# Gate and up products turned to features by tokens, in a Flamingo block on one Trainium2 core

## Chip, cores and metric

The kernel runs on one core of one Trainium2 chip. The metric is device time in microseconds (us) per execution. The kernel before has a median of 458.49 us over 3 runs (458.45, 458.49 and 459.89).

The five engines are named as in the profile: PE is TensorE's matmul stream and PEld its weight loads, DVE is VectorE, ACT is ScalarE, POOL is GpSimd, SP is SyncE, which here only issues DMAs.

## What is computed

The input x has 16 batches of 128 tokens with 512 features. For every batch the kernel computes a gated cross-attention and a gated feed-forward network with Hadamard-rotated, quantized products:

```
x = x + tanh(g_xattn) * attention(layernorm(x), ctx, ctx)      # 32 query heads, 8 key heads, D = 16
x = x + tanh(g_ffn)   * ffn(layernorm(x))

def h_bitlinear(v, w):        # w becomes -1, 0 or 1 times its mean magnitude
    r = hadamard(v)           # along the features, 512 or 2048 of them
    s = 127 / max(max(abs(r)), 1e-5)          # one scale per token
    return (clip(round(r * s), -128, 127) / s) @ ternary(w).T

def ffn(v):                   # w_gate, w_up: 2048 x 512; w_down: 512 x 2048
    return h_bitlinear(silu(h_bitlinear(v, w_gate)) * h_bitlinear(v, w_up), w_down)
```

## The kernel before

One batch of 128 tokens fills the 128 partitions, so there are 16 batches b = 0 to 15, and every batch goes through the same steps. The steps are Python generators: each call runs one up to its next `yield`. A text, `ORDER`, lists 1,489 such calls, and a wrapper (`InOrder`) keeps the instructions of PE, DVE, ACT, POOL and SP in the order in which the list issues them. So each engine works through a fixed queue, and an instruction that waits holds up all that stand behind it on its engine. Steps of several batches are interleaved in the list.

The attention steps of one batch are `moments_q`, `normed`, `q_transposed`, `scores` (PE writes scores `sc`, DVE reduces them to maxima `mx`), `split_max`, `max_turned`, `weights` (PE writes `sT`, ACT takes the exponential `ex`), `summed` (`av`) and `residual` (PE transposes `tpo`, DVE divides, POOL adds into x).

The feed-forward steps of one batch are:

- `moments_h`: mean and variance of x (DVE `stf`, `mvf`), then the inverse root on POOL (`vef`, `rstdf`, `nmf`).
- `in_norm`: ACT writes the normalized row `hn`, POOL does two butterfly levels (`hb`, `hn`).
- `in_turned`, `in_hadamard`: PE transposes 4 blocks (`tph`), a copy to SBUF, PE multiplies by the 128 x 128 Hadamard matrix into `z`.
- `in_scale`, `in_quant`: the maximum per token and its reciprocal (`ae`, `re`), POOL's `dq`, the rounded row `qe` by ACT, a DMA that transposes it (`qTe`).
- `gate.b.m`, `up.b.m` for m = 0, 1: `product` writes a tile of 128 tokens by 1024 features: 8 matmuls with 512 columns each, the activations `qTe` as weights of the array and the ternary weights streaming. ACT takes silu of the gate tile with the token's scale `dq`, giving `sg`; DVE multiplies the up tile, `dq` and `sg` to `h`.
- `hidden_transposed.b.n` for n = 0 to 3: PE turns 4 blocks of `h` (`tpf`), ACT or DVE copies them to SBUF (`hT`).
- `hadamard.b.n`: PE multiplies by the Hadamard matrix into `y`, ACT or DVE copies to `za`.
- `butterfly.b.1/2/4` on DVE (`zb`, `za`), `magnitudes` on ACT, `out_scale` and `out_quant` on DVE (`qf`), a transposing DMA (`qTf`), a cast, and `out_down` (16 matmuls into `yo`, then `res` on DVE and a store).

The last digit of a step such as `hadamard.3.2.1` chooses the engine of its copy: 0 or none is ACT, 1 is DVE.

Other steps are `load_*`, `mag_*`, `mean_*`, `whole_*` and `clipped_*`, which load and ternarize the weights early in the list; `table.i.k`, an activation table load ahead of exponentials (k = 0) or silu (k = 1); and `warm.i.n`, n matmuls whose result nobody reads.

Two PSUM pools matter. `ps_s` has 2 buffers of 1024 values per partition and serves `sc`, `sT`, `gate` and `up`; `ps_x` has 4 buffers of 512 values and serves the rest.

Of the kernel before, what the change touches and what calls it, by code (L numbers as in the profile page):

```python
# [8 lines left out]
F32 = mybir.dt.float32  # L9
BF16 = mybir.dt.bfloat16  # L10
# [13 lines left out]
load_kv0 load_aux warm.0.12 load_x1 load_g.1 fetch.2 moments_q.0 load_g.0 load_g.3 table.0.0  # L24
gates_in load_sel moments_q.0 normed.0 q_transposed.0 load_g.2 q_transposed.0 mag_g.1 scores.0.1
fetch.4 load_u.2 moments_q.1 moments_q.1 warm.1.6 scores.0.1 scores.0.1 normed.1 moments_q.2
scores.0.0 moments_q.2 load_u.3 q_transposed.1 scores.0.0 warm.2.8 q_transposed.1 values_in.1
mag_g.0 scores.0.0 values_in.0 moments_q.3 load_u.1 scores.1.1 mag_g.3 moments_q.3 warm.3.4
scores.1.1 load_u.0 warm.4.2 scores.1.1 split_max.0 max_transposed.0.1 normed.2 max_transposed.0.1
scores.1.0 sel_in mag_g.2 q_transposed.2 scores.1.0 scores.1.0 warm.5.6 mean_g q_transposed.2  # L30
normed.3 weights.0.1 mean_g whole_g.3 whole_g.1 warm.6.8 weights.0.1 weights.0.1 whole_g.0 load_d.0
load_d.3 weights.0.0 moments_q.5 moments_q.5 summed.0.1 mag_u.3.1 weights.0.0 load_d.2 weights.0.0
split_max.1 mag_u.2 scores.2.1 clipped_g.0 max_transposed.1 scores.2.1 summed.0.0.1 max_transposed.1
summed.0.1 residual.0.1 scores.2.1 whole_g.2.1 summed.0.0.1 weights.1.0 residual.0.1 moments_q.4
q_transposed.3.1 weights.1.0 residual.0.0 q_transposed.3.1 weights.1.0 residual.0.0 residual.0.0
mag_u.0 scores.2.0 moments_q.4 summed.1.0 residual.0.1 summed.1.0 scores.2.0 scores.2.0 mag_u.1
residual.1.0 split_max.2 weights.1.1 moments_h.0 clipped_g.3 residual.1.0 moments_h.0
max_transposed.2.1 weights.1.1 fetch.6 mean_u warm.7.8 max_transposed.2.1 mean_u weights.1.1
load_d.1 whole_u.1 in_norm.0 scores.3.1 normed.4 in_norm.0 scores.3.1 whole_u.0.1 q_transposed.4
summed.1.1 in_norm.0 scores.3.1 q_transposed.4 whole_u.3 residual.1.0 normed.5 scores.3.0  # L40
in_turned.0 scores.3.0 in_turned.0 values_in.3 whole_u.2.1 scores.3.0 in_hadamard.0 in_scale.0
split_max.3 weights.2.1 summed.1.1 clipped_u.3 residual.1.1 moments_q.6 moments_q.6 weights.2.1
weights.2.1 max_transposed.3.1 q_transposed.5.1 clipped_g.2 residual.1.1 in_quant.0 weights.2.0
in_quant.0 max_transposed.3.1 moments_q.7 residual.1.1 mag_d.0.1 weights.2.0 values_in.2 summed.2.1
weights.2.0 moments_h.1 moments_h.1 normed.6 weights.3.1 summed.2.1 q_transposed.5.1 clipped_u.1
residual.2.1 weights.3.1 clipped_u.2 q_transposed.6.1 summed.2.0 weights.3.1 residual.2.1 in_quant.0
clipped_g.1 weights.3.0 in_norm.1 mag_d.2.1 summed.2.0 in_norm.1 summed.3.1 fetch.8 weights.3.0
residual.2.0 weights.3.0 in_scale.0 gate.0.0 residual.2.0 residual.2.0 clipped_u.0 mag_d.1.1 up.0.0
table.1.1 gate.0.0 in_norm.1 summed.3.1 mag_d.3 gate.0.1 residual.2.1 q_transposed.6.1 moments_q.7
up.0.0 in_turned.1.1 hidden_transposed.0.1 in_turned.1.1 mean_d up.0.1 moments_h.2  # L50
hidden_transposed.0.1 mean_d moments_h.2 in_hadamard.1 gate.0.1 up.0.1 values_in.4 summed.3.0
values_in.5 summed.3.0 in_scale.1 scores.4.0 moments_q.8 in_scale.1 in_norm.2 hidden_transposed.0.3
scores.4.0 in_quant.1 in_norm.2 hadamard.0.1 residual.3.0 hidden_transposed.0.3 in_quant.1
scores.4.0 hadamard.0.1 hadamard.0.3 moments_q.8 whole_d.0.1 residual.3.0 scores.5.1 residual.3.1
in_norm.2 hadamard.0.3 hidden_transposed.0.2.1 scores.5.1 in_quant.1 in_turned.2 whole_d.3.1
hidden_transposed.0.0 residual.3.1 gate.1.1 scores.5.1 residual.3.0 residual.3.1
hidden_transposed.0.0 moments_q.9 in_turned.2 up.1.1 gate.1.1 moments_h.3 hidden_transposed.0.2.1
normed.7 moments_h.3 in_hadamard.2 up.1.1 hadamard.0.2.1 in_scale.2 scores.4.1 in_quant.2.1
in_scale.2 moments_q.9 hidden_transposed.1.3 in_quant.2.1 hadamard.0.0 in_norm.3 in_norm.3
scores.4.1 scores.4.1 gate.1.0 hadamard.0.0 whole_d.1.1 hadamard.0.2.1 split_max.4 butterfly.0.1  # L60
up.1.0 gate.1.0 in_quant.2.1 in_norm.3 max_turned.4 hidden_transposed.1.2 whole_d.2.1 up.1.0
gate.2.0 clipped_d.1 hidden_transposed.1.2 up.2.0 hidden_transposed.1.3 gate.2.0 butterfly.0.1
butterfly.0.2 hidden_transposed.1.0 hadamard.1.2 up.2.0 hadamard.1.3.1 hidden_transposed.1.0
butterfly.0.2 butterfly.0.4 hadamard.1.2 weights.4.0 in_turned.3 table.2.0 weights.4.0
hidden_transposed.2.0.1 hadamard.1.3.1 hadamard.1.0.1 butterfly.0.4 weights.4.0
hidden_transposed.1.1 in_turned.3 hidden_transposed.2.0.1 weights.4.1 magnitudes.0 clipped_d.3
hadamard.1.0.1 summed.4.0 clipped_d.0 weights.4.1 weights.4.1 in_hadamard.3 out_scale.0
hidden_transposed.1.1 gate.2.1 out_quant.0.1 out_scale.0 hadamard.2.0.1 in_scale.3 out_quant.0.1
table.3.1 gate.2.1 summed.4.1 hadamard.2.0.1 in_scale.3 summed.4.0 scores.5.0 out_quant.0.0.1
values_in.6 in_quant.3 summed.4.1 in_quant.3 residual.4.0 scores.5.0 hadamard.1.1 out_quant.0.0.1  # L70
residual.4.1 residual.4.0 up.2.1 scores.5.0 residual.4.0 in_quant.3 residual.4.1 split_max.5
gate.3.0 up.2.1 hadamard.1.1 out_quant.0.1 butterfly.1.1 butterfly.1.1 residual.4.1 max_turned.5
hidden_transposed.2.1 up.3.0 hidden_transposed.2.1 gate.3.0 out_quant.0.0.1 hadamard.2.1 up.3.0
hidden_transposed.2.3 hadamard.2.1 butterfly.1.2 hidden_transposed.3.0 hidden_transposed.2.3
weights.5.1 butterfly.1.2 hadamard.2.3 table.4.0 weights.5.1 butterfly.1.4 hidden_transposed.3.1
weights.5.1 q_transposed.7 hadamard.2.3 scores.6.0 hidden_transposed.3.0 moments_h.4
hidden_transposed.3.1 summed.5.1 butterfly.1.4 magnitudes.1 scores.6.0 hidden_transposed.2.2
scores.6.0 hadamard.3.0.1 moments_h.4 in_norm.4 out_scale.1 scores.6.1 q_transposed.7 summed.5.1
hadamard.3.1 out_scale.1 in_norm.4 residual.5.1 hadamard.3.1 scores.6.1 scores.6.1 gate.3.1
hidden_transposed.2.2 in_norm.4 hadamard.3.0.1 residual.5.1 hadamard.2.2.1 table.5.1 gate.3.1  # L80
out_quant.1.0 split_max.6 max_turned.6 in_turned.4 weights.5.0 hadamard.2.2.1 butterfly.2.1
out_down.0.0 table.6.0 weights.5.0 in_turned.4 butterfly.2.1 out_quant.1.0 weights.5.0 up.3.1
clipped_d.2 butterfly.2.2 out_down.0.1 up.3.1 out_quant.1.0 out_quant.1.1.1 hidden_transposed.3.3
summed.5.0 weights.6.1 hidden_transposed.3.3 butterfly.2.2 out_quant.1.1.1 summed.5.0 out_down.0.1
butterfly.2.4 hidden_transposed.3.2 weights.6.1 residual.5.0 in_hadamard.4 hidden_transposed.3.2
butterfly.2.4 weights.6.1 hadamard.3.2 residual.5.0 magnitudes.2 weights.6.0 in_scale.4 residual.5.0
residual.5.1 hadamard.3.3 weights.6.0 out_scale.2 out_down.1.0 weights.6.0 out_quant.1.1.1
hadamard.3.3 moments_h.5 in_quant.4 scores.7.1 out_quant.2.1.1 normed.8 moments_h.5 in_quant.4
hadamard.3.2 summed.6.0 scores.7.1 summed.6.1 scores.7.1 out_down.1.1 in_scale.4 values_in.7
summed.6.1 butterfly.3.1 in_norm.5 in_quant.4 in_norm.5 summed.6.0 scores.7.0 out_down.1.1  # L90
residual.6.0 scores.7.0 q_transposed.8 q_transposed.8 in_norm.5 residual.6.1 scores.7.0 gate.4.0
values_in.8 residual.6.1 split_max.7 residual.6.0 out_down.0.1 up.4.0 table.7.1 gate.4.0
out_quant.2.0.1 residual.6.0 gate.4.1 out_quant.2.0.1 up.4.0 residual.6.1 butterfly.3.1 max_turned.7
hidden_transposed.4.1 up.4.1 hidden_transposed.4.1 butterfly.3.2 gate.4.1 in_turned.5 up.4.1
fetch.10 out_quant.2.1.1 hidden_transposed.4.0 hadamard.4.1 hidden_transposed.4.0 butterfly.3.2
butterfly.3.4 in_turned.5 weights.7.0 table.8.0 weights.7.0 weights.7.0 butterfly.3.4
# [164 lines left out]
def flamingo_kernel(  # L261
# [355 lines left out]

    def absmax_scale(b: int, name: str, amax, norm: float):  # L620

# [372 lines left out]
```

## Time and profile before

| | |
|---|---|
| median of the runs | 458.49 us (458.45 to 459.89) |
| span of the profiled execution | 456.3 us, first to last instruction |
| between the span and the median | 2.2 us |
| PE busy | 441.8 us, 97% of the span |
| DVE busy | 416.8 us, 91% |
| ACT busy | 324.2 us, 71% |
| POOL busy | 174.8 us, 38% |
| TensorE clock granted | full (1.000) |

The profile comes from one execution with a span of 456.3 us; no separate device time is listed for that execution, so the 2.2 us that lie around the span are taken from the median. Busy time is the time in which at least one instruction of the engine is under way. Matmuls overlap in the array: the duration of one is longer than the step from it to the next, so costs on PE are taken from steps, not from durations. All lines of the kernel appear as L249, the line of the `InOrder` wrapper, so groups are told apart by the names of their tiles.

### The profile page before, as it was taken

What the parts mean: (1) busy time and instruction counts of PE and PEld (TensorE: products, weight loads), DVE (VectorE), ACT (ScalarE), POOL (GpSimd) and SP (SyncE); (2) the same over time, 40 slices, a digit from 0 to 9 for tenths busy, and PEclk for the clock granted to TensorE, in tenths of its full rate; (3) what the DMA queues carried; (4) which work ended last, traced back from release to release, by engine and by line L of the source; (5) the groups of instructions that cost most, each with busy time, mean ns of one, the idle gap of its engine ahead of it and who ended that gap; (6) DMA issues with size and microseconds to landing.
All of it is one profiled execution on the core that took longest, in us unless ns stands there. A gap on an engine that the chain in (4) does not pass through costs nothing.

```text
span 456.3 us, 8222 instructions
## 1 busy us (share of the span) xinstructions
PE 441.8 (97%) x3191; PEld 266.2 (58%) x3228; DVE 416.8 (91%) x624; ACT 324.2 (71%) x391; POOL 174.8 (38%) x316
## 2 busy tenths in 40 slices
PE   7999899999999999999999999999999999999996
PEld 3534447665665465666555665565556656576862
DVE  4898998999999999999999899989789999989995
ACT  4779897788787677596977878575776748645641
POOL 3315656512241713237274632358152542251000
PEclk9999999999999999999999999999999999999999
DMA  8998220003011153051131513030023503111331
GB/s 283 404 410 272 90 82 13 13 12 59 13 31 29 36 139 83 13 153 33 36 57 36 139 23 70 2 88 18 1 57 47 71 0 62 45 23 37 69 70 69
DMA packets 59350, 36.38 MB, mean 80 GB/s; under 512 B 47792, under 2 KB 52144, under 8 KB 58288
## 3 DMA queue, kind: packets, MB, share of 16 engines
q1 hardware_dynamic: 59312, 35.86, 29.2%
q8 instruction: 25, 0.41, 0.4%
q14 instruction: 13, 0.11, 0.1%
HBM read 20.12 MB, written 4.19 MB: 53 GB/s over the span
## 4 chain that ended last, share of the span: by engine, by line
PE 74%; DVE 10%; DMA 6%; POOL 3%; ACT 3%; issue 2%; SPq 1%; DVEq 0%; POOLq 0%; ACTq 0%
PE y L249 13%; PE yo L249 11%; PE up L249 10%; PE gate L249 10%; PE sT L249 7%; PE tpf L249 6%; PE sc L249 6%; PE av L249 6%; DMA wq_down<-in_w_up 3%; DVE mx L249 3%; PE z L249 3%; PE tpo L249 2%; DVE zb L249 2%; DMA wst_gate<-in_w_gate 2%; DVE h L249 1%
## 5 line engine op out<-in xcount | busy, mean ns | idle before, releaser
L249 DVE TENSOR_REDUCE mx<-sc 128x8 f32<-128x1024 f32 x64 | 75.5, 1217 | 8.6 <-PE sc L249 8.3
L249 PEld LDWEIGHTS <-qTe 128*128 128x128 bf16 x512 | 50.0, 98 | 52.9 <-DVE mx L249 0.8
L249 DVE TENSOR_TENSOR zb<-za 128x1024 f32<-128x1024 f32 (+1 forms) x62 | 72.7, 1198 | 1.4 <-ACT za L249 0.7
L249 PE MATMUL y<-aux,hT 128*128 128x128 f32 x544 | 72.5, 278 | 0.3 <-ACT za L249 0.2
L249 PEld LDWEIGHTS y<-aux,hT 128*128 128x128 f32 x544 | 66.7, 192 | 9.8 <-issue 3.5
L249 ACT ACTIVATE ex<-sT 128x1024 f32<-128x1024 f32 x64 | 62.7, 1026 | 12.1 <-PE sT L249 11.7
L249 PE MATMUL up<-wq_up,qTe 128*128 128x512 bf16 x247 | 60.0, 379 | 0.5
L249 PE MATMUL gate<-wq_gate,qTe 128*128 128x512 bf16 x239 | 59.6, 379 | 0.9
L249 PE MATMUL yo<-wq_down,qTf 128*128 128x512 bf16 x245 | 58.7, 379 | 0.6
L249 POOL TENSOR_TENSOR x<-x,ga 128x256 f32<-128x256 f32 x32 | 30.1, 946 | 47.7 <-DVE ga L249 47.5
L249 DVE SCALAR_TENSOR_TENSOR h<-up,dq,sg 128x1024 f32<-128x1024 f32 x32 | 41.0, 1281 | 7.7 <-ACT sg L249 4.7
L249 ACT ACTIVATE sg<-gate,dq 128x1024 f32<-128x1024 f32 x32 | 35.7, 1116 | 15.5 <-PE gate L249 12.4
L249 PE MATMUL sc<-kb,qT 32*128 32x256 f32 x512 | 40.5, 402 | 1.6 <-ACT qT L249 0.7
L249 PEld LDWEIGHTS <-qTf 128*128 128x128 bf16 x256 | 24.4, 98 | 29.1 <-issue 1.3
L249 PE MATMUL sT<-qT,kb 32*128 32x512 f32 x256 | 40.8, 640 | 0.5 <-DVE h L249 0.2
L249 DVE TENSOR_TENSOR za<-zb 128x1024 f32<-128x1024 f32 (+1 forms) x38 | 39.3, 1059 | 0.2
L249 DVE CUSTOM_DVE_ANT_0 qf<-zb,rf 128x1024 int16<-128x1024 f32 (+1 forms) x32 | 38.9, 1224 | 0.2
L249 ACT COPY hT<-tpf 128x512 f32<-128x512 f32 x45 | 26.1, 591 | 18.2 <-PE tpf L249 16.5
L249 PE MATMUL tpf<-ident,h 128*128 128x128 f32 x256 | 38.0, 277 | 0.4 <-DVE h L249 0.2
L249 PEld LDWEIGHTS tpf<-ident,h 128*128 128x128 f32 x256 | 29.0, 141 | 14.2 <-issue 6.9
L249 POOL TENSOR_TENSOR hb<-hn 128x256 f32<-128x256 f32 x32 | 25.8, 828 | 28.4 <-ACT hn L249 18.1
L249 PEld LDWEIGHTS sc<-kb,qT 32*128 32x128 f32 x512 | 25.1, 184 | 17.8 <-issue 6.5
(128 smaller groups left out, 728.1 us busy)
## 6 DMA issues: line engine op xcount, KB each, us to landing
wst_gate<-in_w_gate SPq DMA_DIRECT2D x4, 1024.0 KB, 9.6
wst_down<-in_w_down SPq DMA_DIRECT2D x4, 1024.0 KB, 12.7
out<-res SPq DMA_DIRECT2D x16, 256.0 KB, 2.2
x<-in_x SPq DMA_DIRECT2D x7, 512.0 KB, 4.1
kb<-in_kb SPq DMA_DIRECT2D x8, 256.0 KB, 4.1
wq_down<-in_w_up SPq DMA_DIRECT2D x2, 1024.0 KB, 14.1
wst_up<-in_w_up SPq DMA_DIRECT2D x2, 1024.0 KB, 15.2
kv<-in_kv SPq DMA_DIRECT2D x8, 128.0 KB, 3.9
```

The source lines that it names most:

```text
L249: ins = f(*args, **kwargs)
```

## The change

Five things are changed together.

1. `product` swaps its operands: the ternary weights are loaded into the array in blocks of 128 x 128, the activations stream with 128 columns. The tile comes out as features by tokens, 32 matmuls with 128 columns in place of 8 with 512. `hidden_transposed` and its copy are gone. The scale of a token now lies along the free axis, so a new step `spread` puts it on all partitions (one matmul with the identity, one copy), and `gate` multiplies by it on DVE, with silu on ACT afterwards, from SBUF to SBUF. `up` multiplies two tensors.
2. `moments_h` and ACT's `hn` are gone. `in_norm` works on x itself; the mean falls out with one zeroed column of the Hadamard matrix (`had_mid`), and the new step `in_power` takes the squares of `z` on ACT with a running sum, then five small instructions on POOL.
3. POOL takes some of the weights' rounding: 4 of the 12 `whole_*` (ACT had 7 of them and has 3 now, DVE keeps 5) and 6 of the 12 `clipped_*` (all were DVE's).
4. For the batches 0 to 13 the end of `out_down` is an ACT copy with the scale and a POOL addition in place of one DVE instruction.
5. Many steps have more `yield`s, and `ORDER` is a new list of 1,696 calls. In it, the choice of engine for `hadamard`'s 64 copies is 57 on ACT and 7 on DVE (before: 42 and 22). The `table` and `warm` steps are the same 26 and 8, in other places; three `warm` steps, with 16 matmuls, stand at the end of the list.

```diff
...
+    had_mid = const.tile([P, P], F32, name="had_mid")
...
         def whole(c: int, k: int = 0):
             w = part[c].bitcast(I16)
-            if k == 0:
-                nc.vector.tensor_scalar(w, st[c], inv, None, ALU.mult)
+            if k == 1:
+                nc.scalar.activation(w, st[c], AF.Copy, scale=inv)
             else:
-                nc.scalar.activation(w, st[c], AF.Copy, scale=inv)
+                (nc.vector, nc.gpsimd)[k // 2].tensor_scalar(w, st[c], inv, None, ALU.mult)
-        def clipped(c: int):
-            nc.vector.tensor_scalar(part[c], part[c].bitcast(I16), -1.0, 1.0, ALU.max, ALU.min)
+        def clipped(c: int, k: int = 0):
+            (nc.vector, nc.gpsimd)[k].tensor_scalar(part[c], part[c].bitcast(I16), -1.0, 1.0, ALU.max, ALU.min)
...
-    def moments_h(b: int):
-        return moments(b, "f")
     def in_norm(b: int):
-        hn = w1.tile([P, KC, P], F32, tag="hn", name=f"hn_{b}")
-        layer_norm(b, "f", hn.rearrange("p c f -> p (c f)"), xs[b])
-        src = hn
+        src = xs[b].rearrange("p (c f) -> p c f", c=KC)
...
+    def in_power(b: int):
+        z = zes[b].rearrange("p c f -> p (c f)")
+        ins[b] = w1.tile([P, E], I16, tag="qe", name=f"qe_{b}")
+        power = tiny.tile([P, 1], F32, tag="power", name=f"power_{b}")
+        nc.scalar.activation(ins[b].bitcast(BF16), z, AF.Square, accum_out=power)
+        yield
+        nc.gpsimd.tensor_scalar(ve, power, 1.0 / E**2, EPS, ALU.mult, ALU.add)
+        yield
+        nc.gpsimd.tensor_tensor(rstd, ve, mhalf, ALU.pow)
+        yield
+        nc.gpsimd.tensor_scalar(dq, wsc[:, 0:2], a, rstd, ALU.mult, ALU.mult)
+        yield
+        nc.gpsimd.tensor_tensor(root, ve, half, ALU.pow)
+        yield
+        nc.gpsimd.tensor_scalar(floor, root, rs["e", b], wsc[:, 3:4], ALU.mult, ALU.mult)
+    def spread(b: int, k: int = 0):
+        row = ps_x.tile([P, P], F32, tag="x", name=f"row_{b}")
+        nc.tensor.matmul(
+            row, lhsT=dqs[b][:, 0:1].to_broadcast([P, P]), rhs=ident, start=True, stop=True
+        )
+        yield
+        rows[b] = w2.tile([P, P], F32, tag="row", name=f"rowb_{b}")
+        copies[k](rows[b], row)
...
     def product(b: int, m: int, w: str):
-        gu = ps_s.tile([P, 2, 512], F32, tag="s", name=f"{w}_{b}_{m}")
-        for j in range(2):
+        gu = ps_s.tile([P, 8, P], F32, tag="s", name=f"{w}_{b}_{m}")
+        for j in range(8):
             for c in range(KC):
                 nc.tensor.matmul(
-                    gu[:, j, :], lhsT=ins[b][:, c, :],
-                    rhs=wq[w][c][:, (2 * m + j) * 512 : (2 * m + j + 1) * 512],
+                    gu[:, j, :],
+                    lhsT=wq[w][c][:, (8 * m + j) * P : (8 * m + j + 1) * P],
+                    rhs=ins[b][:, c, :],
                     start=(c == 0), stop=(c == KC - 1),
                 )
     def gate(b: int, m: int):
         gu = product(b, m, "gate")
         yield
-        sgs[b, m] = w1.tile([P, 2, 512], F32, tag="sg", name=f"sg_{b}_{m}")
-        nc.scalar.activation(sgs[b, m], gu, AF.Silu, scale=dqs[b][:, 0:1])
+        sg = w3.tile([P, 8, P], F32, tag="sg", name=f"sg_{b}_{m}")
+        nc.vector.tensor_tensor(sg, gu, rows[b].unsqueeze(1).to_broadcast([P, 8, P]), ALU.mult)
+        yield
+        nc.scalar.activation(sg, sg, AF.Silu)
     def up(b: int, m: int):
         gu = product(b, m, "up")
         yield
-        h = w2.tile([P, 2, 512], F32, tag="h", name=f"h_{b}_{m}")
-        nc.vector.scalar_tensor_tensor(
-            h, gu, dqs[b][:, 1:2], sgs.pop((b, m)), ALU.mult, ALU.mult
-        )
+        h = sgs.pop((b, m))
+        nc.vector.tensor_tensor(h, gu, h, ALU.mult)
...
-    def hidden_transposed(b: int, n: int, k: int = 0):
-        h = hs[b, n // 2][:, n % 2, :]
-        tp = ps_x.tile([P, 4, P], F32, tag="x", name=f"tpf_{b}_{n}")
-        for c in range(4):
-            nc.tensor.transpose(tp[:, c, :], h[:, c * P : (c + 1) * P], ident)
-        yield
-        hT = w2.tile([P, 4, P], F32, tag="hT", name=f"hT_{b}_{n}")
-        copies[k](hT, tp)
...
     def out_down(b: int, k: int, parts: int = 2):
...
-            nc.vector.scalar_tensor_tensor(res, y, scs[b], xs[b], ALU.mult, ALU.add)
+            if b < 14:
+                nc.scalar.activation(res, y, AF.Copy, scale=scs[b])
+                yield
+                nc.gpsimd.tensor_tensor(res, res, xs[b], ALU.add)
+            else:
+                nc.vector.scalar_tensor_tensor(res, y, scs[b], xs[b], ALU.mult, ALU.add)
             yield
             nc.sync.dma_start(out[b], res)
```

## Prediction

> **What bounds it now.** I read the page first, then the busy time by stretch, the chain of waits, the groups by form, and last single tiles.
>
> ```profile
> PE 441.8 (97%) x3191; PEld 266.2 (58%) x3228; DVE 416.8 (91%) x624; ACT 324.2 (71%) x391; POOL 174.8 (38%) x316
> 100.00:200.00 100.00, 99.40 (x741) 60.19 (x748) 96.52 (x144) 75.34 (x93) 31.34 (x56) 1.00 0.24 56
> 200.00:300.00 100.00, 99.32 (x730) 59.30 (x738) 94.41 (x134) 75.57 (x93) 47.23 (x76) 1.00 0.24 57
> 300.00:400.00 100.00, 98.82 (x716) 60.47 (x724) 92.97 (x139) 70.64 (x84) 41.73 (x65) 1.00 0.24 40
> ```
>
> The columns of the last three lines are the stretch, its length, and the busy time of PE, PEld, DVE, ACT and POOL. PE hardly stops from 100 to 400 us, but DVE is only 3 to 7 us per 100 behind. Work taken from PE alone buys little: DVE is next. The chain agrees: 74% of it is PE, and the transposes that the change removes have their share.
>
> ```profile
> 425.00 1.51 PE gate L249 x7
> 426.51 0.44 PE tpf L249 x4
> 429.11 3.57 PE y L249 x32
> 447.33 0.39 PE L249 MATMUL tpf_q<-ident,qf 128*128 128x128 bf16 x4
> L249 PE MATMUL tpf_q<-ident,qf x16: 219/219/230, 447.3 to 450.6; 128*128 128x128 bf16 x16
> ```
>
> These give steps on PE (start, length, what, count; then a tile's durations, lowest, median, highest). A bf16 matmul with 512 columns takes 1.51/7 = 0.216 us, an f32 transpose 0.44/4 = 0.110, an f32 pass with 128 columns 3.57/32 = 0.112. Four bf16 matmuls with 128 columns, each behind its own weight load, last 0.39 with one lasting 0.219, so their step is (0.39 - 0.219)/3 = 0.057.
>
> ```profile
> L249 DVE SCALAR_TENSOR_TENSOR h<-up,dq,sg 128x1024 f32<-128x1024 f32 x32 | 41.0, 1281 | 7.7 <-ACT sg L249 4.7 <-PE up L249 2.6
> L249 ACT ACT_TABLE_LOAD x26 | 33.4, 1283 | 1.2 <-PEq L984 0.7
> L249 ACT COPY hT<-tpf 128x512 f32<-128x512 f32 x45 | 26.1, 591 | 18.2 <-PE tpf L249 16.5 <-PE y L249 1.4 <-ACT ex L249 0.3
> L249 DVE TENSOR_TENSOR zb<-za x62: 684/1218/1750, 90.4 to 442.6; 128x1024 f32<-128x1024 f32 x58, 128x512 f32<-128x512 f32 x4
> L249 POOL TENSOR_TENSOR x<-x,ga x32: 720/730/1697, 36.9 to 396.3; 128x256 f32<-128x256 f32 x32
> ```
>
> The first three are groups (busy us and mean ns, then idle time before); the last two are tiles. DVE's butterfly goes from its median of 1.218 to 1.750 and POOL's addition from 0.730 to 1.697, so the two do get in each other's way, POOL mostly being the one delayed.
>
> **The change, part by part.** All sums are against the span of 456.3 us; 2.2 us lie around it.
>
> PE. Gone: 256 transposes, 256 x 0.110 = 28.2. The 64 gate and up tiles cost 8 x 0.216 = 1.73 each; they become 32 x 0.057 = 1.82, together +6.1. No run of more than four such matmuls in a row is in the trace. The nearest row on the other side is the f32 pass at 0.112, which has the same 128 columns but the slower weight load (192 ns against 98); the floor is 1.73/32 = 0.054, the streaming of the same columns. I take 0.057, because type and load are the same. `spread`: 16 matmuls of two f32 passes, 3.6. Sum: 441.8 - 28.2 + 6.1 + 3.6 = 423.3.
>
> The Trainium skill speaks against this step: its page "TensorE: Matmul & The Clock Gate", section "Back-to-back issue gap", gives about 81 ns per matmul in a sustained stream of weight loads and matmuls with 128 columns. With it the 64 tiles would cost +55.3 and PE would come to 472.5. The same sentence gives 131 ns for 512 columns, where this trace has 216, so I let the trace decide.
>
> DVE. Gone: 19 copies `hT` 12.7, `stf` and `mvf` 13.8, 14 of the 16 `res` 14 x 0.740 = 10.4, 15 copies of `y` now on ACT 15 x 0.681 = 10.2, 6 clips 6 x 0.682 = 4.1, other copies on balance 2.6: together 53.8. New: the gate tile's multiplication, 32 times, between 1.218 (butterfly, SBUF) and 1.281 (`h`, same PSUM tile); I take 1.25, 40.0. `h` itself drops to that too, -1.0. Nine copies of the token row, 0.28 each from the cast of 256 values (0.283): 2.5. Sum: 416.8 - 53.8 + 41.5 = 404.5.
>
> ACT. Gone: `hT` 26.1, `hn` 13.1, four `whole` 8.0, silu from SBUF some 1.9. New: 15 copies of `y` 8.9, 16 squares 14.1 (0.693 as `qe` on the same tile, and 0.19 for the accumulator's read), 14 scaled `res` 9.7, seven token rows 2.2, other copies 3.9. Sum: 313.9. Then the table loads. Before, all 26 loads are the 26 `table` steps, and every one stands where the function changes. Following ACT's queue in the new list, the function still changes 26 times, but 25 of the uses find the wrong table behind the last `table` step. So there are between 26 loads (misplaced ones dropped) and 51, and ACT has between 313.9 and 313.9 + 25 x 1.283 = 346.0. I take 51, since each of the 26 steps did become a load before. ACT then is at 79% of 440 us: mostly hidden, not everywhere.
>
> POOL. Gone: `vef`, `rstdf`, `nmf`, `dq`, 30.6. New: five small instructions per batch, 0.47 + 0.58 + 0.46 + 0.58 + 0.46, 40.8 in all; 14 additions of 512 values, twice 0.730, 21 (to 27 by the mean of 0.946); ten roundings of 2048 values, each between 2.1 (four of `m_pad`'s memset of 512 at 0.524) and 9.8 (sixteen of `v_pad`'s 128 at 0.610). I take 4, below the addition's rate (eight times 0.730 = 5.8) as there is one input less: 40. Sum 246, from 227 to 310, under POOL's span either way. The cover is the long wait that POOL has now. Without it: five of the ten stand ahead of the first gate product, where the list has 32 us of other POOL work in 64 us; at 9.8 they would add 32 + 49 - 64 = 17 us. DVE's butterflies may be held by the long additions; the whole excess of the 58 butterflies over their median is 0.8 us now, so I price this at 0 to 4 and take 1, within the rounding of the sum.
>
> Waits. `gate` on DVE waits for PE and the token row; silu waits for it; `h` waits for silu. Behind the waiting `h` stand maxima, butterflies and rounding, on which PE's `ps_s` buffers and the stores depend. In the new list DVE has 0.7 to 11.2 us of other work between a tile's scale and its `h`, and only in 2 of 32 cases less than silu's 1.1; a table load of 1.28 ahead of silu is covered in most. The chain of `in_power` (a square, three POOL steps, one matmul, one copy, some 3 us) stands ahead of the gate tile's multiplication in the list, for several batches by one step only, so part of the 19 below is its wait. On SP, stores are moved behind later loads and transposes; their issue takes about 0.5 each, and SP is nowhere near full. The three `warm` steps at the end take 16 x 0.216 = 3.5 beside the last `res` and store (3.7 from the last `yo` to the end now): 0 to +1, I take 0.
>
> Sum of the parts. DVE becomes the fuller engine relative to what stops it. Its idle time now is 39.5: 10.9 up to 60 us (loads), 5.6 from 440 us on, 23.0 between. Head and tail stay. Of the 23.0, waits for PE are the largest part (`mx` for `sc` 8.3 over the run), and PE gets slack; against that stands the new silu in the middle of DVE's work. I keep four fifths, 19. 404.5 + 10.9 + 5.6 + 19 = 440, with 2.2 around it 442. From PE's side: 423.3 with its present idle of 14.5 gives 437.8, 440 with the 2.2. Both ends meet, so I predict 442, with 434 to 452 as this case's own range.
>
> **Rivals.**
>
> 1. *Slower: the short matmuls don't keep their step.* 2048 matmuls pay every ns. PE reaches its present 441.8 when the step is (1.73 x 64 + 24.6)/2048 = 0.066 us; from there the transposes are paid back. Halfway to the f32 row, 0.084, PE has 441.8 - 28.2 + 61.4 + 3.6 = 478.6, and with 14.5 and 2.2 the time is 495. For it: no long run in the trace, and twice 32 instructions per tile where 16 were. Against it: the measured 0.057, and weight loads of 98 ns that lie beside matmuls. Chance 0.10.
> 2. *ACT gives it back.* Between the first products of batches 3 and 4 the list holds 44 us of ACT work with all loads, against 37 on PE and 39 on DVE; ahead of the first product ACT has 58 (54 before). With two fifths of 25 x 1.283 = 32.1 us on the path, 13, the time is 455; it is level with now when half of it, 16, is. For it: exponentials empty the two `ps_s` buffers, so a load ahead of them stops PE. Against it: ACT idles 29% now, and a load can run while ACT waits. Chance 0.22, of it 0.10 faster, 0.05 same, 0.07 slower.
> 3. *Better packing.* With DVE's middle idle at 10 the time is 433. For it: PE's slack of some 18 us. Against it: three engines above 79%, in fixed queues. Chance 0.10.
>
> The forecast itself has 0.58. A measurement tells some 0.3% (1.4 us) from no change. Faster: 0.58 + 0.10 + 0.10 = 0.78; same 0.05; slower 0.10 + 0.07 = 0.17. The range 430 to 463 leaves out rival 1 and the edges of the others.
>
> **What would show it.** Steps of the gate and up matmuls at 0.057, 32 per tile; `tpf`, `hT`, `hn`, `stf` gone; DVE busy near 404 and above 91% of the span, PE near 423; some 50 table loads; POOL's roundings near 4 us each. The prediction is wrong if DVE's idle time rises well above 36 us, with `h` waiting for silu or `ex` behind table loads, or if the matmul step exceeds 0.066.

## The result: 508.7 us, a tenth slower

The changed kernel has a median of 508.66 us over 4 runs (507.2 to 511.5), against 459.18 us for the kernel before in the same comparison (4 runs). The ratio is 1.1085, with a 95% interval of 1.1048 to 1.1123. The prediction, 442 us, was wrong by sign and lies 67 us off, outside its range.

The profiled execution has a span of 505.4 us. These lines answer to those shown of before. First the page's busy times, then the busy time by stretch (stretch, its length, busy PE, PEld, DVE, ACT, POOL with counts, granted clock, DMA share, GB/s):

```profile
PE 450.8 (89%) x4520; PEld 318.1 (63%) x4540; DVE 425.8 (84%) x576; ACT 342.0 (68%) x421; POOL 311.0 (62%) x359
```

```profile
0.00:100.00 100.00, 77.01 (x625) 44.14 (x626) 72.80 (x105) 60.29 (x75) 74.95 (x93) 0.86 0.49 177
100.00:200.00 100.00, 88.80 (x962) 66.42 (x962) 84.12 (x104) 73.96 (x89) 73.00 (x69) 0.97 0.11 25
200.00:300.00 100.00, 93.83 (x995) 66.62 (x998) 88.68 (x119) 74.31 (x92) 59.15 (x74) 0.98 0.22 57
300.00:400.00 100.00, 93.43 (x951) 65.13 (x960) 87.42 (x117) 68.79 (x89) 54.03 (x74) 0.97 0.23 50
```

No engine is full any more. From 100 to 400 us PE has 89 to 94 us per 100 where it had 99, DVE 84 to 89 where it had 93 to 97. DVE's idle time is 505.4 - 425.8 = 79.6 us, against 39.5 before. PE's busy time is 450.8 us, above the 441.8 of before, though the change takes work off it. Part of that is the clock, which was full before. Now its mean is 0.956, so some 22 us' worth of full clock are lost, in six stretches, the longest in this one (the third column from the end is the granted clock):

```profile
20.00:40.00 20.00, 18.30 (x106) 8.23 (x107) 14.05 (x24) 13.56 (x18) 13.48 (x6) 0.66 0.96 371
```

Added up over the trace, 44.4 us of the span run at half clock, and PE is busy for 36.0 of them.

The steps of the new products, from the chain of waits (start, length, what, count):

```profile
272.68 3.57 PE gate L256 x64
```

3.57/64 = 0.056 us, as predicted. The Trainium skill's 81 ns per matmul of this kind ("TensorE: Matmul & The Clock Gate", "Back-to-back issue gap"), which the prediction had weighed, isn't seen here, in runs of 32 or 64.

Groups by form (busy us, mean ns, idle time before them and what ended it):

```profile
L256 DVE TENSOR_TENSOR sg<-gate,rowb 128x1024 f32<-128x1024 f32 x32 | 38.9, 1218 | 4.2 <-PE gate L256 3.9
L256 DVE TENSOR_TENSOR sg<-up,sg 128x1024 f32<-128x1024 f32 x32 | 38.6, 1216 | 13.8 <-ACT sg L256 12.2 <-PE up L256 1.4
L256 ACT ACT_TABLE_LOAD x48 | 61.6, 1283 | 2.2 <-PEq L1040 0.7 <-PE sT L256 0.7
L256 DVE TENSOR_TENSOR zb<-za 128x1024 f32<-128x1024 f32 x58 | 78.4, 1384 | 7.1 <-ACT za L256 6.6
L256 POOL TENSOR_SCALAR wq_down<-wq_down 128x2048 bf16<-128x2048 int16 x3 | 21.2, 7079 | 0.1
L256 POOL TENSOR_SCALAR wq_down<-wst_down,inv_down 128x2048 int16<-128x2048 f32 x2 | 10.9, 5444 | 0.0
```

The second line is `h`: it waits 12.2 us for silu, before 4.7. DVE's butterfly takes 1384 ns on average, its median being still 1.22 us. A clip on POOL takes 7.08 us, a rounding 5.44. The waits that have grown (who waits for whom: us in total, times, longest); the first line is of before, the others of the changed kernel:

```profile
DVE mx L249 <- PE sc L249: 8.3, 12, 2.2
DVE mx L256 <- PE sc L256: 24.5, 18, 6.0
ACT ex L256 <- PE sT L256: 20.5, 21, 3.3
PEld tph L256 <- POOL hn L256: 12.8, 6, 7.8
DVE sg L256 <- ACT sg L256: 12.2, 8, 2.9
```

DVE waits for PE's scores 24.5 us, before 8.3, and PE waits for POOL's `hn`. PE in turn waits for all three: its idle time that ended with another engine's work is 17.7 us for ACT, 15.2 for POOL and 14.4 for DVE, where before it was 3.1, 1.3 and 3.6 (added up over the two traces).

And how POOL and DVE meet, from the timeline (start, length, engine, instruction):

```profile
73.09 7.57 POOL L256 TENSOR_SCALAR wq_up<-wq_up 128x2048 bf16<-128x2048 int16 x1
75.51 5.70 DVE L256 TENSOR_SCALAR wq_up<-wq_up 128x2048 bf16<-128x2048 int16 x1
...
423.97 2.11 POOL L256 TENSOR_SCALAR dq<-wsc,ae,rstdf 128x2 f32<-128x2 f32 x1
```

DVE's clip, whose least duration is 0.69 us, starts inside POOL's and ends at 81.21, 0.55 us after POOL's end at 80.66. In the third line an instruction on two values per partition takes POOL 2.11 us. The Trainium skill ("SBUF — State Buffer", "SBUF: two separate sides") says that certain DVE instructions and POOL's take a common pair of ports as an exclusive lock for a whole instruction; the first two lines agree with it.

### The profile page after: what moved, and what is told of

Its sections match the earlier page's. It is cut to its first block, busy times and chain, and to the rows that moved or that the text cites. A ratio compares the mean times of both kernels' runs of the same rounds, so it can differ in the third digit from the quotient of the medians.

```text
span 505.4 us, 10935 instructions
## 1 busy us (share of the span) xinstructions
PE 450.8 (89%) x4520; PEld 318.1 (63%) x4540; DVE 425.8 (84%) x576; ACT 342.0 (68%) x421; POOL 311.0 (62%) x359
## 4 chain that ended last, share of the span: by engine, by line
PE 28%; DVE 21%; ACT 11%; POOL 5%; issue 4%; DMA 3%; ACTq 0%; DVEq 0%; POOLq 0%
PE y L256 6%; DVE zb L256 5%; PE yo L256 5%; DVE qf L256 4%; PE sT L256 4%; PE gate L256 4%; DVE za L256 4%; DVE mx L256 3%; DVE sg L256 3%; ACT L256 3%; PE sc L256 3%; PE up L256 2%; ACT ex L256 2%; DMA qTf<-qf 2%; PE av L256 2%
## 5 line engine op out<-in xcount | busy, mean ns | idle before, releaser
L256 DVE TENSOR_REDUCE mx<-sc 128x8 f32<-128x1024 f32 x64 | 75.4, 1216 | 24.6 <-PE sc L256 24.5
L256 PE MATMUL y<-aux,sg 128*128 128x128 f32 x544 | 75.2, 285 | 1.7 <-DVE sg L256 1.7
L256 PEld LDWEIGHTS y<-aux,sg 128*128 128x128 f32 x544 | 67.4, 196 | 13.5 <-issue 9.4
L256 PE MATMUL gate<-qTe,wq_gate 128*128 128x128 bf16 x1024 | 63.0, 222 | 2.0 <-DVE mx L256 1.2
L256 PEld LDWEIGHTS <-wq_gate 128*128 128x128 bf16 x1024 | 60.6, 99 | 6.0 <-issue 4.7
L256 PE MATMUL up<-qTe,wq_up 128*128 128x128 bf16 x1024 | 61.6, 219 | 2.2 <-ACT ex L256 1.2
L256 PEld LDWEIGHTS <-wq_up 128*128 128x128 bf16 x1024 | 59.0, 98 | 3.3 <-issue 2.5
L256 DVE TENSOR_TENSOR sg<-up,sg 128x1024 f32<-128x1024 f32 x32 | 38.6, 1216 | 13.8 <-ACT sg L256 12.2
L256 ACT COPY za<-y 128x512 f32<-128x512 f32 x53 | 30.2, 590 | 26.1 <-PE y L256 24.1
L256 DVE TENSOR_TENSOR sg<-gate,rowb 128x1024 f32<-128x1024 f32 x32 | 38.9, 1218 | 4.2 <-PE gate L256 3.9
L256 ACT ACTIVATE sg<-sg 128x1024 f32<-128x1024 f32 x32 | 33.6, 1057 | 11.7 <-DVE sg L256 11.4
```

The costliest lines, as they stand in the source:

```text
L256: ins = f(*args, **kwargs)
```

## The experiments

Theories, by the letters used in the expectations: A, POOL's roundings hold the head, and DVE by the ports; B, table loads hold ACT; C, the new order and its longer chains; D, half clock in the head; E, POOL's other long instructions hold DVE; F, DVE is simply full; G, the layout frees PE; H, the chain gate, DVE scale, silu, `h` stops the fixed queues; R, the token row does. Every time is the median of its runs; "list" is the text `ORDER`. e9, e10, e11 and e14 to e17 leave out the token's scale, wholly or in part, so they don't compute the block; they show only what a piece costs.

**The roundings, the tables, the clock (e1 to e5).** The ten steps on POOL go back to DVE (`clipped`) and ACT (`whole`):

```diff
-clipped_g.0.1 ... whole_g.2.2
+clipped_g.0 ... whole_g.2.1
```

> The changed kernel with its ten POOL roundings back on the engines of before (6 clips on DVE, 4 whole on ACT), the list of steps otherwise as changed. Theory A (POOL's roundings of 5.4 to 7.6 us each hold up the head, and DVE by the shared port): the first gate product comes some 20 us earlier, DVE's butterflies fall from 1.38 to near 1.24 us mean, time 478 to 487 us. Theory B (table loads hold up ACT): at least 500 us. Theory C (the new order and the longer chain gate, scale, silu, up are what costs): 495 to 505 us.

The 26 table steps are left out, so that each load stands where the function changes:

```diff
-table.0.0 ... table.25.1
```

> The changed kernel without the 26 table steps; loads then stand only where an activation needs another table, about 26 in place of 48. Theory A: under 8 us gained, 500 to 507. Theory B: 22 loads of 1.28 us are 28 us, most of them on the path: 480 to 488. Theory C: 503 to 509.

Both together:

> Both at once: roundings back and no table steps. Theory A: 474 to 484 us. Theory B: 478 to 486. If the two add up and nothing else costs, 455 to 462. Theory C: 490 to 503 us.

The same ten roundings on POOL, in the kernel and list of before:

> The kernel before, in its own order, with the same ten roundings put on POOL. Theory A: the ten roundings cost there too, 15 to 25 us more than before, 474 to 484. Theories B and C: within 5 us of before, 457 to 464.

And e3 with the three `warm` steps of the list's end put ahead of the first scores:

> The third experiment's kernel (roundings back, no table steps) with the three warm steps moved from the end of the list to the head, ahead of scores.0.0, scores.1.1 and scores.1.0. Theory D (PE waits in the head, the granted clock halves for 17 us, and that delays the first gate products by some 8 us): the halved stretch at 17 to 34 us is gone and the time is 470 to 474. If the head waits for loads and DVE anyway: 478 to 482.

Measured: e1 490.0, ratio to before 1.068 (1.0663 to 1.0696), 18.7 less than the change and between the ranges of A and C. e2 507.83, 1.1065 (1.1024 to 1.1106), no difference that can be told. e3 479.88, 1.0497 (1.0433 to 1.0561), with 26 loads in place of 48: 10.1 us less than e1, though the tables alone gave nothing. e4 499.04, 1.0878 (1.0848 to 1.0908): 40.4 us for ten roundings in the list of before, where POOL had been at 38%, and above A's 484. e5 477.88, 1.0429 (1.0399 to 1.046), not told apart from e3. The half clock of e3 from 16.7 to 33.8 us is gone in e5, so D is small in the head. What half clock costs over the whole run no run shows.

A is therefore the first large cause. Its two parts are seen in the trace. One is POOL's queue, in the timeline of the changed kernel:

```profile
27.45 14.12 POOL L256 TENSOR_SCALAR wq_gate<-wq_gate 128x2048 bf16<-128x2048 int16 x2 [2.50 <-DMA wst_up<-in_w_up]
41.56 5.45 POOL L256 TENSOR_SCALAR wq_gate<-wst_gate,inv_gate 128x2048 int16<-128x2048 f32 x1
47.08 1.04 POOL L256 TENSOR_SCALAR vea<-mva 128x1 f32<-128x1 f32 x1
...
53.33 1.40 POOL L256 TENSOR_TENSOR hn<-hn 128x256 f32<-128x256 f32 x2
...
54.10 1.37 PE L256 MATMUL tph<-ident,hn 128*128 128x128 f32 x4 [7.60 <-POOL hn L256]
```

Two clips and a rounding hold the queue from 27.45 to 47.0 us. The norms, the addition into x and `hn` stand behind them, and PE waits 7.60 us for `hn`. The first gate product starts at 82.6 us in the change, at 75.4 in e1 and at 64.2 before: 7.2 of e1's 18.7 us are gained by then, not the 20 that A expected, and the rest later. The other part is DVE instructions that last longer. Adding up by how much each exceeds the median of its group (same tiles, operation and shape) gives 23.7 us for the change, 2.7 for before, 14.9 for e4. In the change, 23.4 of it lie on instructions that overlap one of POOL's, but only 10.1 on those that overlap a rounding. The excess remains 13.4 in e1 and 14.9 in e5, so over half of it lies beside other POOL work (E).

**The last addition (e6).** e3 with `res` of all batches on DVE, as before:

```diff
-            if b < 14:
+            if b < 0:
```

> The third experiment's kernel with the end of out_down on DVE for all batches, as before: no POOL addition of 512 values, 14 x 0.74 us more on DVE. Theory E (POOL's long additions hold DVE's butterflies by the shared port, 1.31 us mean against 1.23): butterflies back to 1.24, time 472 to 480. Theory F (DVE is simply full): 10 us more, 486 to 492.

Measured 482.85, 1.0555 (1.0497 to 1.0613). The intervals with e3 overlap, so the fourth part of the change gains some 3 us or nothing. Without POOL's 14 additions DVE's excess is 10.7 us, where e3 has 15.2, and the time doesn't follow: neither E's range nor F's holds the result.

**The parts in the list of before (e7, e8, e12).** e7 is the kernel of before with the first part of the change alone; e8 has the functions of the first and second part. e12 has the second alone.

```diff
 # e7: product, gate, up as in the change; hidden_transposed gone; behind dq, in in_scale's second call:
+        row = ps_x.tile([P, P], F32, tag="x", name=f"row_{b}")
+        nc.tensor.matmul(row, lhsT=dqs[b][:, 0:1].to_broadcast([P, P]), rhs=ident, start=True, stop=True)
+        rows[b] = w2.tile([P, P], F32, tag="row", name=f"rowb_{b}")
+        nc.scalar.copy(rows[b], row)
```

> The kernel before, in its own list, with the first change alone: gate and up products as features by tokens, no hidden_transposed, spread after dq, DVE scaling and ACT silu in the gate step's second call. Only the floor of the maximum is left without the token's scale. DVE gains 40 us of scaling and loses 13 of copies, PE loses some 20. Theory F (DVE is the bound): DVE busy near 445, time 465 to 475. Theory G (a layout without transposes frees PE and that is what counts): 445 to 456. Theory H (gate, scale, silu, up in one row stops the fixed queues): 480 or more, with DVE idle rather than busy.

> The changed kernel's arithmetic for products and norm (first and second change) in the list of before, with the steps mapped one to one, roundings and the end of out_down as before. DVE busy should be near 432. Theory C (the new list is what costs in the third experiment): 450 to 462. Theory F: 455 to 466. Theory H: 475 or more, near the third experiment's 480.

> Kernel and list of before with the second part of the change alone: no moments_h, no hn on ACT, the norm from the squares of the transform (a square on ACT, three small POOL steps up to dq), gate and up as before with transposes. e8 minus e7 was +20 us. If that was the chain to dq itself (square, three POOL steps, ahead of silu), this run shows it too: 470 to 480. If it was the token row behind it (e8's PE waits for dq, 20.9 and 25.2 us), which is not here, the run stays within 5 us of before, 454 to 464; DVE loses its 13.8 us of stf and mvf, which F would count as up to 10 us of gain, 448.

Measured: e7 510.26, 1.1126 (1.109 to 1.1161), in H's range; e8 530.14, 1.1571 (1.1534 to 1.1609); e12 469.22, 1.0237 (1.0201 to 1.0274). With the functions of e8 the new list (with its choice of engines for the copies, and no table steps) gives 482.85 (e6), the one of before 530.14, above every range of the expectation but H's open one. So C's range for e8, 450 to 462, fails. That doesn't clear the new list: 25 us in e7 belong to the row as I placed it in the list of before (e16, below), and in e8 PE waits 20.9 us for the same `dq`. Of the second part, the steps up to `dq` cost 10 us in e12, less than the 20 between e7 and e8, and just under the 470 to 480 for the chain to `dq`. The first part, which by the prediction's sum takes 18.5 us off PE (28.2 gone, 6.1 and 3.6 new), loses 52 there. The waits of e7, and its timeline at one place (idle time before the instruction in brackets):

```profile
ACT sg L218 <- DVE sg L218: 79.0, 30, 5.3
PEld row L218 <- POOL dq L218: 14.9, 10, 4.1
PE row L218 <- POOL dq L218: 11.4, 7, 3.9
```

```profile
225.92 1.22 DVE L218 TENSOR_TENSOR sg<-up,sg 128x1024 f32<-128x1024 f32 x1
...
227.19 0.70 PE L218 MATMUL sc<-kb,qT 32*128 32x256 f32 x4 [1.29 <-DVE sg L218]
...
228.19 1.22 DVE L218 TENSOR_TENSOR sg<-gate,rowb 128x1024 f32<-128x1024 f32 x1
...
229.43 1.06 ACT L218 ACTIVATE sg<-sg 128x1024 f32<-128x1024 f32 x1 [4.89 <-DVE sg L218]
229.45 2.08 PE L218 MATMUL sc<-kb,qT 32*128 32x256 f32 x12 [1.57 <-DVE sg L218]
```

Here PE writes the next scores only when DVE has emptied the up tile and then the gate tile, because gate, up, `sc` and `sT` share the two buffers of `ps_s`. Before, ACT emptied the gate tile; now DVE empties 8 of the 12 tiles of a batch, where it was 6. So DVE, the second fullest engine, stands in front of PE at one more tile. Whether that costs more than the work itself, e15 below has to say.

**The 62 us taken apart (e11, e16, e14, e15).** e11 is e7 without row and multiplication:

```diff
-        nc.vector.tensor_tensor(sg, gu, rows[b].unsqueeze(1).to_broadcast([P, 8, P]), ALU.mult)
-        yield
-        nc.scalar.activation(sg, sg, AF.Silu)
+        nc.scalar.activation(sg, gu, AF.Silu)
```

> Like e7 (kernel and list of before with the gate and up products as features by tokens, without transposes; 510.3 us), without the token row and without DVE's multiplication by it: silu from PSUM on ACT, at its place in the list of before, without the token's scale. What is left of the layout is the gain alone: 256 transposes and their copies are gone, the short matmuls are there. G (the layout frees PE): PE's demand falls from 425 to about 411, DVE's busy time to some 401, and the time lies below before, at 436 to 450. F and H say the same, both put the loss on the multiplication or its waits. If the short matmuls, with twice the weight loads, cost by themselves, the time lies above 458; if the loss of e7 had another cause, it stays above 490.

e16 gives back the row alone, e14 the row and an eighth of the multiplication; e15 adds to e11 the same amount of work on DVE at another place.

```diff
 # e14
+        nc.vector.tensor_tensor(gu[:, 0, :], gu[:, 0, :], rows[b], ALU.mult)
         nc.scalar.activation(sg, gu, AF.Silu)
 # e15, in butterfly, for both halves
+        for _ in range(2 if step == 1 or (b < 2 and step == 2) else 1):
             nc.vector.tensor_tensor(dlo, lo, hi, ALU.add)
```

> e11 with the token row spread as in e7 (one matmul with the identity, a copy on ACT, 16 times), which nobody reads. F and H: 448 to 456 (3.6 us on PE, 16 x 0.3 = 5 us on ACT, POOL's dq waited for by PE). R: 470 and up.

> e11 with the token row as in e7 (one matmul of two passes, one copy on ACT, 16 times) and a multiplication by it on DVE of the first 128 of the gate tile's 1024 columns, in place in PSUM, ahead of silu; seven eighths of the gate tile stay without scale. DVE gets some 32 x 0.25 = 8 us in place of 37. F: 450 to 460, the share of the work. H: the order of waits is e7's, so most of the 62 us is back, 480 to 500. R: the row alone, 470 and up, and e16 the same.

> e11 with 32 additional instructions on DVE of the size of the gate tile's multiplication (1.22 us each, 39 us in all), but outside the chain from gate to h: the first butterfly level of the batches 0 to 13 is computed twice, and the second of batches 0 and 1. The result of them is that of e11. F: 485 to 510, all of e7's loss comes from the work. H: DVE's busy time becomes 444, with its idle time at the ends (16.5) the time can't be under 460; 460 to 472.

Measured: e11 447.77, 0.976 (0.9739 to 0.978); e16 472.78, 1.0305 (1.0277 to 1.0334); e14 484.62, 1.0564 (1.0509 to 1.0619); e15 486.76, 1.0605 (1.0586 to 1.0624). The pages of e11 and e15:

```profile
PE 427.5 (96%) x4508; PEld 305.3 (68%) x4508; DVE 404.7 (91%) x605; ACT 299.2 (67%) x346; POOL 185.3 (42%) x332
```

```profile
PE 443.7 (92%) x4508; PEld 313.5 (65%) x4508; DVE 444.4 (92%) x637; ACT 298.8 (62%) x346; POOL 194.7 (40%) x332
```

G holds: the layout by itself takes 11 us off, and PE's busy time falls from 441.8 to 427.5, at full clock. Then the steps to e7: +25.0 for the row, +11.8 for the eighth of the multiplication, +25.6 for the rest, together 62.5. e16 lies in R's range, e14 in H's and R's. All three theories have a share, and none is the whole. The eighth adds 6.6 us to DVE's busy time and costs 11.8, the rest adds 29.5 and costs 25.6. So beyond the row it is mostly DVE's work (F), and some 5 us of it can be the order of the waits (H). The row makes PE wait for POOL's `dq` (e16):

```profile
PEld row L218 <- POOL dq L218: 11.8, 9, 4.0
PE row L218 <- POOL dq L218: 8.0, 5, 3.4
```

In the changed kernel, whose list has the row elsewhere, PE's waits hold none for `dq`; so the row's price seems to be that of my placing, though no run moves the row alone. These waits aren't all of the 25 us: from e11 to e16 PE's idle time grows from 18.2 to 30.6 us and its busy time from 427.5 to 441.7, with 17.1 us of the span at half clock where e11 has none.

e15 is the plainest: 39 us of work on DVE outside every chain from gate to `h` cost 39 us of time, though DVE had 445.7 - 404.7 = 41 us of idle time. F's 485 to 510 was right and H's 460 to 472 wrong; that idle time could not be filled. In e15 ACT empties the gate tile, and PE still waits 22.7 us for DVE, where e7 has 20.8 and e11 4.8. So the price of e7's multiplication doesn't need the buffer as its reason: DVE's work at another place costs as much. Part of the 39 us is again the clock: 18.8 us of e15's span run at half clock.

**The multiplication in the new list (e9, e10, e17).** All start from e5. e9 leaves it out, with silu in its place; e10 multiplies an eighth in PSUM there; e17 keeps every step in its place and multiplies an eighth into a small tile, which silu reads eight times:

```diff
 # e17
-        nc.vector.tensor_tensor(sg, gu, rows[b].unsqueeze(1).to_broadcast([P, 8, P]), ALU.mult)
+        cut = w3.tile([P, P], F32, tag="cut", name=f"cut_{b}_{m}")
+        nc.vector.tensor_tensor(cut, gu[:, 0, :], rows[b], ALU.mult)
         yield
-        nc.scalar.activation(sg, sg, AF.Silu)
+        nc.scalar.activation(sg, cut.unsqueeze(1).to_broadcast([P, 8, P]), AF.Silu)
```

> Like e5 (new list, the ten roundings back on DVE and ACT, no table steps, three warm steps in the head; 477.9 us), with the gate tile's multiplication by the token row on DVE left out: ACT takes silu straight from PSUM, without the token's scale, in the place where DVE's multiplication stood. The token row is still spread, but read by nobody. DVE loses 32 x 1.217 = 38.9 us. F (DVE is simply full): its 418.6 become 380, and with e5's idle time of 58.5 the time is about 439. H (the chain PE gate, DVE scale, ACT silu, DVE h stops the fixed queues): DVE's idle time falls as well, to the 36 to 40 of before, and PE becomes the bound: its demand of 412 plus the 25 that it lost before, 437 and up, at most 445. If neither is the cause, and the list or the power chain holds the engines, the time stays above 465.

> Like e9, but DVE multiplies the first 128 of the gate tile's 1024 columns by the token row, in place in PSUM, ahead of ACT's silu from PSUM; seven eighths of the gate tile stay without their scale. The order of waits is that of the change (PE, DVE, ACT, DVE), the work on DVE is about 0.25 us in place of 1.217, so DVE loses some 31 us. F (DVE full): within 10 us of e9, 439 to 450. H (the waits, not the work): most of what e9 gains is lost again, 462 to 475. Between 450 and 462 both have a share, in proportion.

> e5 (new list, roundings back, no table steps, warm steps in the head; 477.9) with the gate tile's multiplication on DVE cut to 128 of the 1024 columns, into a small tile; ACT's silu reads that small tile eight times over, so its work, its place and all waits are e5's, and DVE alone frees the gate tile. Seven eighths of the gate products are not used. DVE gets some 32 x 1.0 = 31 us less. F (DVE's work as such): 447 to 460. H or the order of the list as the bound (the fixed queues wait on each other at other places): 468 to 482. If it is as fast as F says, e9's failure to gain came from silu's new place.

Measured: e9 481.43, 1.0523 (1.0469 to 1.0576); e10 492.2, 1.0749 (1.0687 to 1.081); e17 474.34, 1.0332 (1.0302 to 1.0362). F falls here, and so does H's 437 to 445 for e9: it gains nothing on e5, the case that its expectation gives to the list or the power chain. e10 is 10.8 us above e9 for 7.6 us more on DVE, about as the eighth did in the list of before. e17 takes 418.6 - 391.8 = 26.8 us off DVE and gains 3.5, within its 468 to 482 for H or the list. Its page shows why:

```profile
PE 440.4 (93%) x4520; PEld 311.6 (66%) x4540; DVE 391.8 (83%) x582; ACT 318.8 (67%) x403; POOL 242.1 (51%) x349
```

PE is at 93% and nobody else above 83%. In this list DVE's work doesn't set the time; what is taken off becomes idle time. e9 shows it too, in DVE's waits for PE's up tile (first e5, then e9):

```profile
DVE sg L253 <- PE up L253: 1.1, 4, 0.4
DVE sg L253 <- PE up L253: 27.7, 20, 7.0
```

What of the 20 us between e5 and before is the power chain (10 us in e12's list) and what is the order, these runs don't separate. Nor do they clear the new list: without the multiplication, the list of before gives 447.8 (e11) and the new one 481.4 (e9). Besides the lists, these two differ in the power chain, the row and the end of `out_down`.

**A version that beats both (e13).** e11 shows what the layout is worth if the scale costs nothing. A token's scale can be applied while tokens still lie on partitions:

```diff
         nc.scalar.activation(q, z, AF.Copy, scale=rs.pop(("e", b)))
+        nc.scalar.activation(q.bitcast(BF16), q, AF.Copy, scale=dqs[b][:, 0:1])
         yield
         ...
         nc.sync.dma_start(qT, q, transpose=True)
         yield
         ins[b] = qT.bitcast(BF16)
-        copies[k](ins[b], qT)
```

> Like e11 (list of before, products as features by tokens, no transposes, silu straight from PSUM), with the token's scale in place: ACT multiplies the rounded row by dq, a scale per partition while tokens are still on the partitions, and writes bf16, ahead of the DMA that transposes it; the copy from int16 to bf16 behind that DMA falls away. The scaled row is rounded to bf16, which the kernel before does not do. The constant ratio of up's and gate's scales goes into down's scale. One instruction on ACT is exchanged for one of the same size, DVE has what it has in e11, so F, H and R all give 448, 444 to 453; if the later start of the DMA (one ACT instruction of some 0.7 us and the wait for POOL's dq) shows, up to 460. Below before (459) in each case but the last.

Beyond these lines, `dq` is issued one call earlier, and the constant ratio of the two scales moves into the one of `out_down`. Measured 452.69 over 5 runs, ratio 0.9866 (0.9846 to 0.9887): 1.3% faster than before and 11% than the change. It has the old list, no row, no multiplication, no power chain and no roundings on POOL, and it rounds the scaled row to bf16, which neither kernel does. By span it is 450.0 - 445.7 = 4.3 us above e11, of which PE's busy time has 1.5 and its idle time 2.8.

## Why the prediction was wrong

The prediction's own sum for DVE divides the 66.7 us between 442 and 508.7, to 0.2: busy 425.8 for 404.5 (+21.3), idle 79.6 for 35.5 (+44.1), around the span 3.3 for 2.2 (+1.1, mostly because the profiled execution was 1.5 us faster than the median).

- **The failing step is the idle time between head and tail.** "I keep four fifths, 19" supposed that DVE's waits would shrink with PE's slack. They came to 50.6 us. Up to 60 us it is 21.8 in place of 10.9, in the tail 7.2 in place of 5.6. DVE's waits for `sc` rose from 8.3 to 24.5 and those of `h` for silu from 4.7 to 12.2. Without the roundings on POOL and the misplaced table loads (e5) the middle still has 38.9, with these two waits:

```profile
DVE mx L253 <- PE sc L253: 13.1, 16, 3.3
DVE sg L253 <- ACT sg L253: 9.9, 6, 2.9
```

So 28.8 of the 49.5 us that the change loses to before come from the roundings and the loads (e1, then e3). The cause of the last 20 stays open: some 10 can be the power chain (e12), and the share of the new list isn't known. That DVE empties the gate tile is seen in e7, but no run shows it as the cause.
- **The slack that was to come from PE didn't.** PE is busy 450.8 us for a forecast of 423.3, and idle 54.6 for 14.5. The sum has no term for the clock: 36.0 us of PE's busy time ran at half clock, some 18 us more than at full clock (an estimate, half of 36.0). Some 9 us are left over, and e11, at full clock, has 8 of the kind: 427.5, where the sum without `spread` gives 419.7. "Both ends meet" took two sums with this same slack for a confirmation.
- **DVE's work was right, its price wasn't.** By medians it is 425.8 - 23.7 = 402.1, against 404.5. The term that failed is the contention with POOL, "1, from 0 to 4": the excess grew from 2.7 to 23.7. I took it from the butterflies of before, which met 0.73 us additions, and carried it over to instructions of 5 to 7 us, and to more of the short ones: only 10.1 us of the excess lie beside a rounding. POOL's small steps last longer as well: the five per batch take 58.3 us in all, not 40.8.
- **The roundings had no cover.** Ten took 4 x 5.45 and 6 x 7.15, some 65 us, within the bounds but over the 4 each that I took. "The cover is the long wait that POOL has now" was a mean over the run; from 40 to 80 us POOL is busy for 38.6 of 40 us. e1 measured 18.7, near the 17 that I had named as the price without cover and left out of the forecast, but that is luck: the 17 holds at 9.8 us each. The five ahead of the first gate product took 32.6 us, and the same sum then gives 32 + 32.6 - 64 = 0.6. It weighed POOL's busy time and not what waits behind each rounding.
- **Right:** the matmul step of 0.056; the loss of `tpf`, `hT`, `hn`, `stf`; 48 table loads for 51 and ACT at 342.0 for 346.0; the direction of the layout (e11, 11 us). The sign I had set for being wrong, DVE's idle time well above 36 us with `h` waiting for silu, is what the profile shows.
- **The rivals.** Rival 1 (longer steps) didn't occur. Rival 2 (ACT gives it back, 13 us) has about the right size once the roundings are gone, 10 between e1 and e3, and nothing before that; that the loads were hidden behind longer waits there is likely, but not shown. Rival 3 didn't occur. The case that came, POOL's roundings and idle time that grew on PE and DVE alike, was no rival.

## What to carry to other kernels

Before work is moved to an engine, don't count that engine's idle time as a reserve because it is idle: ask what each wait is for. Here, with PE at 96% and DVE at 91% in fixed queues, 39 us more on DVE cost 39 us, though it had 41 us of idle time; in another list, 27 us less gave 3.5. A mean over the run is no cover for a long instruction either: ask what stands behind it in its own queue, at that place. And a scale can be applied where it lies along the partitions, ahead of the transposition, rather than on the widest tile, if the extra rounding to bf16 is acceptable.

## What was not expected of the hardware

- Clipping 2048 int16 values per partition to bf16 takes 7.08 us on POOL and 0.69 on DVE; f32 to int16 takes 5.44 on POOL, 1.28 on DVE, 2.0 on ACT.
- A DVE clip that takes 0.69 us at its shortest lasted 5.70 beside such a clip on POOL, and POOL instructions on one or two values lasted over 2 us beside DVE's butterflies.
- PE ran at half clock for 44.4 us of the changed kernel's span, and for none of the span of before or of e11.
- Pairs of a 128-column bf16 matmul and its own weight load keep 0.056 us in runs of 64.
